# Graph attention, layer 3 in column tiles of TensorE: values in 64 columns, totals in 32

## The chip, the cores and the metric

One core of a Trainium2 chip runs the whole program. The metric is the device time of one execution in microseconds; executions of one kernel agree within about 0.2%. The profile is one execution, with every instruction of every engine.

## The reference

Sixteen independent graphs of 1024 nodes with 256 features go through four layers of graph attention with a layer norm ahead of each and a residual behind. Layers 0 to 2 have one head of 256; layer 3, the one that the change touches, has 4 heads of 64:

```python
weight = sum over types t of (adj == t+1) * (e_src[..., t, :, None] + e_dst[..., t, None, :])
weight = leaky_relu(weight, 0.01)
weight = where(adj == 0, NEG, weight)
attention = softmax(weight, axis=-1)             # per head, 1024 x 1024
dst = einsum('bhij,bhje->bhie', attention, h) + bias
out = relu(dst) + h                              # then a layer norm per head
```

The kernel does not form the softmax. It forms unnormalised weights, multiplies them with the values and with a column that gives their total, and divides afterwards.

## The kernel before

Two batches are in work at a time, as two streams of Python generators. A stream yields an estimate of what it has just traced, and the stream that is behind goes next; the second starts `LAG` later. In layer 3 a stream makes the weights of one head on VectorE (8 tiles of 128 sources x 1024 targets) while TensorE multiplies those of the head before:

```python
EXT = [3, 3, 3, 3 * H]
LAG = 120.0
...
def accumulator(b):                       # in PSUM, two per stream
    return psum.tile([P, HALF], F32, name=f"acc{b % 2}")
...
for n in range(H * NH):                   # 4 heads x 2 halves of 512 targets
    h, g = divmod(n, NH)
    if g == NH - 1:
        behind = weigh3(h + 1)            # VectorE: weights of the next head
        yield from start(behind, b)
    accT = accumulator(b)[: E + 1, :]
    for j in range(NI):                   # 8 blocks of sources
        ...
        nc.tensor.matmul(                 # 64 value columns and the total
            accT, V3[:, j, h, :], weights[h * NI + j][:, ts(g, HALF)],
            start=(j == 0), stop=(j == NI - 1),
        )
        ...
        yield 0.9
    ...
    sums = wide.tile([E + 1, HALF], F32, name="sums")
    nc.scalar.copy(sums, accT)
    ...
    acc = psum.tile([P, NG, E + 1], F32, name="misc")
    for i in range(NG):                   # turn: targets back on partitions
        nc.tensor.transpose(acc[:, i, :], sums[:, ts(i, P)], ident[: E + 1, : E + 1])
    inv = small.tile([P, NG], F32, name="inv4")
    inverse(inv, acc[:, :, E])
    nc.vector.tensor_mul(
        y[:, ts(g, NG), h, :], acc[:, :, :E], inv.unsqueeze(2).to_broadcast([P, NG, E])
    )
```

Of the kernel before, what the change touches and what calls it, by code (L numbers as in the profile page):

```python
# [32 lines left out]
F32 = mybir.dt.float32  # L33
# [8 lines left out]
P = 128  # L42
# [17 lines left out]
def short_path(ctx: ExitStack, tc: tile.TileContext, ins: dict, out: bass.AP, bad: bass.AP):  # L60

    nc = tc.nc
    x, adj = ins["x"], ins["adj"]
    B, N, D = x.shape
    H, T, E = ins["L3_a_src"].shape
    NI = N // P
    NK = D // P
    HALF = 512
    NH = N // HALF
    NG = HALF // P  # L70
    EXT = [3, 3, 3, 3 * H]
    LAG = 120.0

    const = ctx.enter_context(tc.tile_pool(name="const", bufs=1))
    nodes = ctx.enter_context(tc.tile_pool(name="nodes", bufs=3))
    adjs = ctx.enter_context(tc.tile_pool(name="adjs", bufs=4))
    wide = ctx.enter_context(tc.tile_pool(name="wide", bufs=2))
    psum = ctx.enter_context(tc.tile_pool(name="psum", bufs=2, space=bass.MemoryType.PSUM))
    dram = ctx.enter_context(tc.tile_pool(name="dram", bufs=1, space=bass.MemoryType.DRAM))

    ident = const.tile([P, P], F32, name="ident")
# [2 lines left out]
    nc.vector.memset(minus_half, -0.5)  # L84
    ones = const.tile([P, P], F32, name="ones")
    nc.vector.memset(ones, 1.0)

    squares = const.tile([P, B, NI], F32, name="squares")
    inverses = const.tile([P, B, NI], F32, name="inverses")
# [16 lines left out]
    def load(b: int):  # L106


        narrow = narrows[b % 2]
        rows = narrow.bitcast(U8).rearrange("(c t q) j -> c q t j", t=2, q=P)  # L110
        for c in range(NI // 2):
            cast = nc.gpsimd.dma_start(
                rows[c], adj[b, ts(c, 2 * P), :].rearrange("(q t) j -> q t j", t=2)
            )
            tc.keep_in_program_order(cast)
        if b < 2:
            fetch_nodes(b)
        yield

        mask = masks[b] = nodes.tile([P, NI // 2, N, 2], U8, name="mask")  # L120
        for c in range(NI // 2):
            turn = nc.sync.dma_start_transpose(
                mask[:, c].rearrange("p n t -> p (n t)").bitcast(BF), narrow[:, ts(c, P)]
            )
            tc.keep_in_program_order(turn)
            yield
        if b > 1:
            fetch_nodes(b)
            yield
# [20 lines left out]
    small = ctx.enter_context(tc.tile_pool(name="small", bufs=6))  # L150
# [109 lines left out]
    def accumulator(b: int) -> bass.AP:  # L260
        return psum.tile([P, HALF], F32, name=f"acc{b % 2}")
# [54 lines left out]
    def start(behind, b: int):  # L316

        for t in behind:
            if row_taken == [b]:
                return  # L320
            yield t

    def inverse(inv: bass.AP, total: bass.AP):

        nc.vector.tensor_scalar_max(inv, total, TINY)
        nc.vector.reciprocal(inv, inv)  # L326
# [12 lines left out]
    def batch(b: int):  # L339
# [3 lines left out]
        coming = load(b + 2) if b + 2 < B else iter(())  # L343
# [39 lines left out]
        def attend(l: int, V: bass.AP, finish, then: int):  # L383

            weights = []
            behind = weigh(
                b, lambda i: V[:, i, D + 2 : D + 3], lambda j: V[:, j, D + 1 : D + 2],
                ALU.min if l == 1 else ALU.max, weights,
            )
            yield from start(behind, b)  # L390
            following = begin(then) if then < 3 else begin3()
            steps = iter(())
            accs = {}

            def product(i: int, j: int):
                if j == 0:
                    accs[i] = accumulator(b)[:, : D + 1]
                nc.tensor.matmul(  # L398
                    accs[i], weights[j][:, ts(i, P)], V[:, j, : D + 1],
                    start=(j == 0), stop=(j == NI - 1),  # L400
                )


            for j in range(NI):
                next(behind)
                product(0, j)
                product(1, j)
                if b == 0 and j == NI - 1:


                    next(preparing)
                    if l == 0:
                        next(loading[1])
                    next(preparing, None)
                yield 0.9
            for _ in behind:
                pass
            for i in range(NI):
                if i > 1:
                    for j in range(NI):  # L420
                        product(i, j)
                acc = accs.pop(i)
                finish(i, acc)
                if l == 2:
                    next(testing)
                if i != 0:
                    yield 3.6
                if i % 2 == 1:

                    yield from steps  # L430
                    steps = project(b, then, xb, i // 2, following[1])
                yield from islice(steps, 1)
            yield 1.0
            yield from steps
            return following[0]
# [23 lines left out]
        V3 = yield from attend(2, V, finish, 3)  # L459
# [3 lines left out]
        y = single.tile([P, NI, H, E], F32, name="y")  # L463
        normed = []
        shape = [P, NI, E]

        def center(h: int):

            yh = y[:, :, h, :]
            head = ts(h, E)  # L470
            nc.gpsimd.tensor_add(yh, yh, bias[:, head].unsqueeze(1).to_broadcast(shape))  # L471
            nc.vector.scalar_tensor_tensor(yh, yh, 0.0, h3[:, :, head], op0=ALU.max, op1=ALU.add)
            mean = small.tile([P, NI], F32, name="mean")
            nc.vector.tensor_reduce(mean, yh, AX.X, ALU.add)
            nc.vector.tensor_scalar_mul(mean, mean, 1.0 / E)
            nc.vector.tensor_sub(yh, yh, mean.unsqueeze(2).to_broadcast(shape))
            square = wide.tile(shape, F32, name="wide", bufs=1)
            nc.scalar.activation(square, yh, AF.Square)
            var = small.tile([P, NI], F32, name="var")
            nc.vector.tensor_reduce(var, square, AX.X, ALU.add)  # L480
            return yh, head, inverse_root(var, NI, L3_EPS, 1.0 / E)

        def rescale(yh: bass.AP, head, rstd: bass.AP):
            nc.vector.tensor_mul(yh, yh, rstd.unsqueeze(2).to_broadcast(shape))
            nc.gpsimd.tensor_mul(yh, yh, gamma[:, head].unsqueeze(1).to_broadcast(shape))
            nc.gpsimd.tensor_add(yh, yh, xb[:, :, head])

        weights = []

        def weigh3(h: int):  # L490
            if h == H:
                return iter(())
            return weigh(
                b, lambda i: ex[:, i, 2 * H + h : 2 * H + h + 1],
                lambda j: ex[:, j, H + h : H + h + 1], ALU.max, weights,
            )

        behind = weigh3(0)
        yield from start(behind, b)
        for n in range(H * NH):  # L500
            h, g = divmod(n, NH)
            if g == NH - 1:

                behind = weigh3(h + 1)
                yield from start(behind, b)

            accT = accumulator(b)[: E + 1, :]
            for j in range(NI):
                if n == 0:
                    next(behind)  # L510
                nc.tensor.matmul(  # L511
                    accT, V3[:, j, h, :], weights[h * NI + j][:, ts(g, HALF)],
                    start=(j == 0), stop=(j == NI - 1),
                )
                if n > 0:
                    next(behind, None)
                yield 0.9
            for _ in behind:
                pass
            sums = wide.tile([E + 1, HALF], F32, name="sums")  # L520
            nc.scalar.copy(sums, accT)  # L521
            next(coming, None)
            yield 0.5
            acc = psum.tile([P, NG, E + 1], F32, name="misc")
            for i in range(NG):
                nc.tensor.transpose(acc[:, i, :], sums[:, ts(i, P)], ident[: E + 1, : E + 1])  # L526
            inv = small.tile([P, NG], F32, name="inv4")
            inverse(inv, acc[:, :, E])
            nc.vector.tensor_mul(  # L529
                y[:, ts(g, NG), h, :], acc[:, :, :E], inv.unsqueeze(2).to_broadcast([P, NG, E])  # L530
            )
            yield 0.5
            if g == NH - 1:
                if h > 0:
                    rescale(*normed.pop())
                normed.append(center(h))
                yield 1.0
        for _ in coming:
            pass
        rescale(*normed.pop())  # L540
# [8 lines left out]
    def stream(first: int):  # L549
        for _ in loading[first]:  # L550
            yield 2.0
        for b in range(first, B, 2):
            yield from batch(b)
# [3 lines left out]
    next(preparing)  # L557
    streams = [[0.0, stream(0)], [LAG, stream(1)]]
    while streams:
        ahead = min(streams, key=lambda s: s[0])  # L560
        t = next(ahead[1], None)
# [381 lines left out]
```

## Time and profile before

| | before |
|---|---|
| time, median | 3114.9 us |
| TensorE busy | 2982 us (96%) |
| VectorE busy | 2338 us (75%) |
| layer 3's matmuls (line 511), records | 2048, one each 429 ns |
| mean granted clock of TensorE | 0.995 |

The lines behind this table are in the prediction. "Busy" of TensorE rests on modelled ends: successive matmuls overlap in it. To cost TensorE's work one takes the spacing from start to start, not the mean duration. Adding up the starts' spacings by line gives, for before, 1404 us for layers 0 to 2 (line 398), 890 for layer 3 (511), 471 for projections (289), 149 and 129 for two kinds of transposes (282, 306) and 38 for layer 3's turning (526).

### The profile page before, as it was taken

To read this page: it belongs to the slowest core of one execution; us is meant where nothing else is said; L and a number is where in the kernel's file an instruction comes from. 1 tells how busy PE (TensorE), PEld (TensorE's weight loads), DVE (VectorE), ACT (ScalarE), POOL (GpSimd) and SP (SyncE) were. 2 spreads that over 40 slices of the span, in tenths; PEclk is the share of its full clock that TensorE was granted. 3 is DMA by queue.
4 is the path that set the end of the run, shared out by engine and by line. 5 is a ranking of instruction groups with operands and counts; after the bars stand their busy time and mean duration, and the time that the engine had idled before them with its cause. 6 is when DMAs were issued, how large, how long until landed. Compare 5 with 4: busy or idle time off the path is not lost.

```text
span 3112.0 us, 35525 instructions
## 1 busy us (share of the span) xinstructions
PE 2981.7 (96%) x12678; PEld 2047.5 (66%) x12678; DVE 2337.8 (75%) x5234; ACT 737.1 (24%) x1729; POOL 1081.2 (35%) x1405
## 2 busy tenths in 40 slices
PE   7899999999999999999999999999999999999986
PEld 5676756767566675766757667575666767667652
DVE  6678787777877768787786877778777787777856
ACT  1221312223131231312213122231322313122130
POOL 2323433244242333424244242342423434243332
PEclk9999999999999999999999999999999999999998
DMA  8112212022121122111122120221212222001010
GB/s 126 28 28 41 41 14 54 14 41 41 28 44 19 33 41 41 35 20 48 21 41 41 14 54 14 41 41 28 45 15 37 41 35 41 7 28 27 1 28 15
DMA packets 116872, 105.52 MB, mean 34 GB/s; under 512 B 73681, under 2 KB 91217, under 8 KB 116689
## 3 DMA queue, kind: packets, MB, share of 16 engines
q0 software_dynamic: 44256, 81.80, 16.2%
q1 hardware_dynamic: 72432, 21.37, 3.5%
q8 instruction: 103, 1.69, 0.2%
q14 instruction: 81, 0.66, 0.1%
HBM read 153.49 MB, written 33.55 MB: 60 GB/s over the span
## 4 chain that ended last, share of the span: by engine, by line
PE 78%; DVE 15%; POOL 3%; ACT 2%; issue 1%; DMA 1%; SPq 0%; ACTq 0%; POOLq 0%; DVEq 0%
PE acc L398 35%; PE acc L511 25%; PE acc L289 11%; DVE weights L310 8%; PE misc L282 3%; PE row L306 2%; ACT adj_i L141 1%; PE misc L526 1%; POOL y L471 1%; POOL rstd L257 1%; DVE V L355 1%; DVE stats L269 1%; POOL x_b L337 1%; DVE centered L274 1%; ACT below L333 1%
## 5 line engine op out<-in xcount | busy, mean ns | idle before, releaser
L398 PE MATMUL acc<-V,weights 128*128 128x257 f32 x6144 | 1449.3, 383 | 38.0 <-DVE weights L310 29.8
L398 PEld LDWEIGHTS acc<-V,weights 128*128 128x128 f32 x6144 | 1141.6, 190 | 348.6 <-DVE weights L310 100.6
L511 PE MATMUL acc<-weights,V 128*65 128x512 f32 x2048 | 955.9, 592 | 2.0 <-DVE weights L310 1.7
L310 DVE SCALAR_TENSOR_TENSOR weights<-row,ex,mask 128x1024 f32<-128x1024 f32 x512 | 627.8, 1274 | 6.1 <-PE row L306 5.6
L257 POOL TENSOR_TENSOR rstd<-rstd,minus_half 128x2 f32<-128x2 f32 (+1 forms) x320 | 299.5, 936 | 943.1 <-DVE rstd L256 930.7
L289 PE MATMUL acc<-W,hT 128*128 128x259 f32 (+1 forms) x2048 | 515.4, 389 | 26.0 <-ACT hT L284 14.8
L310 DVE SCALAR_TENSOR_TENSOR weights<-row,V,mask 128x1024 f32<-128x1024 f32 x384 | 482.0, 1274 | 46.6 <-PE row L306 46.6
L511 PEld LDWEIGHTS acc<-weights,V 128*65 128x65 f32 x2048 | 273.9, 138 | 361.0 <-issue 312.5
L289 PEld LDWEIGHTS acc<-W,hT 128*128 128x128 f32 x2048 | 379.2, 191 | 138.4 <-ACT hT L284 38.2
L337 POOL TENSOR_TENSOR x_b<-x_b,above 128x256 f32<-128x256 f32 x256 | 196.5, 771 | 427.5 <-DVE above L336 345.1
L333 ACT ACTIVATE below<-acc,inv 128x256 f32<-128x256 f32 x256 | 120.3, 473 | 771.4 <-DVE inv L326 623.6
L269 DVE BATCH_NORM_STATS2 stats<-x_b 128x6 f32<-128x256 f32 x512 | 207.6, 418 | 92.9 <-POOL x_b L337 83.5
L284 ACT COPY hT<-misc 128x512 f32<-128x512 f32 x256 | 146.7, 586 | 344.7 <-PE misc L282 344.6
L471 POOL TENSOR_TENSOR y<-y,bias 128x512 f32<-128x512 f32 x64 | 82.8, 1294 | 406.9 <-DVE y L529 323.5
L274 DVE TENSOR_SCALAR centered<-x_b,mv 128x256 f32<-128x256 f32 x512 | 192.6, 384 | 15.7 <-PE misc L282 12.2
L351 ACT ACTIVATE V<-acc,rstd 128x3 f32<-128x3 f32 x384 | 98.2, 262 | 418.0 <-PE acc L289 418.0
L282 PEld LDWEIGHTS misc<-ident,centered 128*128 128x128 f32 x1024 | 124.1, 141 | 109.7 <-issue 49.0
L282 PE MATMUL misc<-ident,centered 128*128 128x128 f32 x1024 | 162.7, 278 | 31.1 <-DVE centered L274 21.6
L335 DVE TENSOR_SCALAR above<-acc,inv 128x256 f32<-128x256 f32 x256 | 122.5, 481 | 84.4 <-ACT below L333 83.8
L521 ACT COPY sums<-acc 65x512 f32<-65x512 f32 x128 | 74.5, 582 | 409.6 <-PE acc L511 409.6
L355 DVE TENSOR_SCALAR V<-acc,rstd,V 128x256 f32<-128x256 f32 x256 | 133.4, 538 | 37.7 <-ACT V L351 34.9
L141 ACT ACTIVATE adj_i<-adj_i,minus_half 128x1024 bf16<-128x1024 bf16 x128 | 145.8, 1139 | 20.0 <-DMA adj_i<-in_adj_dram 20.0
(69 smaller groups left out, 1870.3 us busy)
## 6 DMA issues: line engine op xcount, KB each, us to landing
adj_i<-in_adj_dram POOLq DMA_DIRECT2D x128, 256.0 KB, 3.9
narrow<-in_adj_dram POOLq DMA_DIRECT2D x64, 256.0 KB, 9.4
out_dram<-y POOLq DMA_DIRECT2D x32, 512.0 KB, 4.3
x_b<-in_x_dram POOLq DMA_DIRECT2D x14, 1024.0 KB, 5.6
x_b<-in_x_dram SPq DMA_DIRECT2D x2, 1024.0 KB, 7.2
mask<-narrow SPq DMA_TRANSPOSE x64, 3.7
W<-in_L_gnn_W_dram SPq DMA_DIRECT2D x3, 256.0 KB, 6.1
weights<-in_L_gnn_a_dram SPq DMA_DIRECT2D x3, 256.0 KB, 7.9
```

The lines of the kernel that those rows point to most:

```text
L141: square = nc.scalar.activation(adj_i, adj_i, AF.Square, bias=minus_half, accum_out=squares[:, b, i : i + 1])
L257: nc.gpsimd.tensor_tensor(r, r, minus_half.to_broadcast([P, n]), op=ALU.pow)
L269: nc.vector.bn_stats(stats, xb[:, 2 * pair + n, :])
L274: nc.vector.tensor_scalar(centered[:, n, :], xb[:, 2 * pair + n, :], mv[:, n, 0:1], 0.0, op0=ALU.subtract, op1=ALU.max,)
L282: nc.tensor.transpose(turned[:, k, ts(n, P)], centered[:, n, ts(k, P)], ident)
L289: nc.tensor.matmul(projected, hT[:, k, ts(n, P)], W[l][:, k, :], start=(k == 0), stop=(k == NK - 1),)
L310: nc.vector.scalar_tensor_tensor(w, r, c(j), masks[b][:, j // 2, :, j % 2], op0=op, op1=ALU.mult)
L333: nc.scalar.activation(below, acc[:, :D], AF.Exp, scale=inv)
L337: nc.gpsimd.tensor_add(xi, xi, above)
L355: nc.vector.tensor_scalar(V[:, i, :D], projected[:, :D], rstd, V[:, i, D : D + 1], op0=ALU.mult, op1=ALU.mult,)
L398: nc.tensor.matmul(accs[i], weights[j][:, ts(i, P)], V[:, j, : D + 1], start=(j == 0), stop=(j == NI - 1),)
L511: nc.tensor.matmul(accT, V3[:, j, h, :], weights[h * NI + j][:, ts(g, HALF)], start=(j == 0), stop=(j == NI - 1),)
```

## The change

Only 65 of the array's 128 columns hold something in line 511. The change divides the array: the 64 value columns go into a tile of 64 columns, and the two halves of targets into the two tiles at once; the one total column is spread over a tile of 32 columns, and two source blocks x two halves go into the four tiles at once. The partial totals of two tiles are added when they are turned, by a small matrix `parts`.

```diff
-    LAG = 120.0
+    LAG = 111.0
+    QUAD = P // 4
...
+    parts = const.tile([P, NH], F32, name="parts")      # picks and adds the four tiles' rows
...
+        for h in range(H):
+            acc = accumulator(b)
+            total = accumulator(b)
+            size = NI if h == 0 else NI // 2
+            for first in range(0, NI, size):
+                for j in range(first, first + size):
+                    if h == 0:
+                        next(behind)
+                    for g in range(NH):
+                        nc.tensor.matmul(
+                            acc[ts(g, E), :], V3[:, j, h, :E], weights[h * NI + j][:, ts(g, HALF)],
+                            start=(j == 0), stop=(j == NI - 1),
+                        )
+                    yield 0.9
...             # (sums = copy of acc; the next head's weights are begun)
+                for j in range(first, first + size, 2):
+                    for n, g in ((n, g) for n in range(2) for g in range(NH)):
+                        nc.tensor.matmul(
+                            total[ts(2 * g + n, QUAD), :],
+                            V3[:, j + n, h, E:].to_broadcast([P, QUAD]),
+                            weights[h * NI + j + n][:, ts(g, HALF)],
+                            start=(j == 0), stop=(j == NI - 2),
+                        )
+                    ...
+                    yield 0.9
...
+            turned = psum.tile([P, NG, NH], F32, name="misc")
             for i in range(NG):
-                nc.tensor.transpose(acc[:, i, :], sums[:, ts(i, P)], ident[: E + 1, : E + 1])
+                nc.tensor.matmul(turned[:, i, :], totals[:, ts(i, P)], parts, start=True, stop=True)
+            inv = small.tile([P, NH, NG], F32, name="inv8")
+            inverse(inv, turned.rearrange("p i g -> p g i"))
+            turned = psum.tile([P, NG, NH, E], F32, name="misc")
+            for i in range(NG):
+                nc.tensor.transpose(
+                    turned[:, i].rearrange("p g e -> p (g e)"), sums[:, ts(i, P)], ident
+                )
...             # (one multiply by inv for both halves)
```

More of the change, by code (lines that the diff above doesn't have):

```diff
@@ L86, in short_path @@
     nc.vector.memset(ones, 1.0)
+    parts = const.tile([P, NH], F32, name="parts")
+    nc.vector.memset(parts, 0.0)
+    for t in range(4):
+        nc.vector.memset(parts[t * QUAD : t * QUAD + 1, t // 2 : t // 2 + 1], 1.0)
     squares = const.tile([P, B, NI], F32, name="squares")
@@ L499, in batch @@
         yield from start(behind, b)
-        for n in range(H * NH):
-            h, g = divmod(n, NH)
-            if g == NH - 1:
-                behind = weigh3(h + 1)
-                yield from start(behind, b)
-            accT = accumulator(b)[: E + 1, :]
-            for j in range(NI):
-                if n == 0:
-                    next(behind)
-                nc.tensor.matmul(
-                    accT, V3[:, j, h, :], weights[h * NI + j][:, ts(g, HALF)],
-                    start=(j == 0), stop=(j == NI - 1),
-                )
-                if n > 0:
+        for h in range(H):
[12 more added lines that the diff above has]
+                    yield 0.9
+                if first + size == NI:
+                    for _ in behind if h == 0 else ():
+                        pass
+                    sums = wide.tile([P, HALF], F32, name="sums")
+                    nc.scalar.copy(sums, acc)
+                next(coming, None)
+                if first == 0:
+                    behind = weigh3(h + 1)
+                    yield from start(behind, b)
+                for j in range(first, first + size, 2):
[6 more added lines that the diff above has]
+                        )
@@ L516, in batch @@
                     next(behind, None)
-                yield 0.9
+                    next(behind, None)
+                    yield 0.9
             for _ in behind:
                 pass
-            sums = wide.tile([E + 1, HALF], F32, name="sums")
-            nc.scalar.copy(sums, accT)
+            totals = wide.tile([P, HALF], F32, name="sums")
+            nc.scalar.copy(totals, total)
             next(coming, None)
             yield 0.5
-            acc = psum.tile([P, NG, E + 1], F32, name="misc")
+            turned = psum.tile([P, NG, NH], F32, name="misc")
@@ L525, in batch @@
             for i in range(NG):
-                nc.tensor.transpose(acc[:, i, :], sums[:, ts(i, P)], ident[: E + 1, : E + 1])
-            inv = small.tile([P, NG], F32, name="inv4")
-            inverse(inv, acc[:, :, E])
+                nc.tensor.matmul(turned[:, i, :], totals[:, ts(i, P)], parts, start=True, stop=True)
+            inv = small.tile([P, NH, NG], F32, name="inv8")
+            inverse(inv, turned.rearrange("p i g -> p g i"))
+            turned = psum.tile([P, NG, NH, E], F32, name="misc")
@@ L529, in batch @@
+            for i in range(NG):
+                nc.tensor.transpose(
+                    turned[:, i].rearrange("p g e -> p (g e)"), sums[:, ts(i, P)], ident
+                )
             nc.vector.tensor_mul(
-                y[:, ts(g, NG), h, :], acc[:, :, :E], inv.unsqueeze(2).to_broadcast([P, NG, E])
+                y[:, :, h, :].rearrange("p (g i) e -> p g i e", g=NH),
+                turned.rearrange("p i g e -> p g i e"),
+                inv.unsqueeze(3).to_broadcast([P, NH, NG, E]),
@@ L531, in batch @@
             )
             yield 0.5
-            if g == NH - 1:
-                if h > 0:
-                    rescale(*normed.pop())
-                normed.append(center(h))
-                yield 1.0
+            if h > 0:
+                rescale(*normed.pop())
+            normed.append(center(h))
+            yield 1.0
         for _ in coming:
```

## The prediction

> **What bounds the kernel now.** I read the page's busy table first, then the strip of 40 slices, the chain that ended last, the costliest groups, and last the timeline of TensorE in a stretch where layer 3 of one stream runs beside layers 0 to 2 of the other.
>
> ```profile
> span 3112.0 us, 35525 instructions
> PE 2981.7 (96%) x12678; PEld 2047.5 (66%) x12678; DVE 2337.8 (75%) x5234; ACT 737.1 (24%) x1729; POOL 1081.2 (35%) x1405
> ...
> PE   7899999999999999999999999999999999999986
> PEclk9999999999999999999999999999999999999998
> ...
> PE 78%; DVE 15%; POOL 3%; ACT 2%; issue 1%; DMA 1%; SPq 0%; ACTq 0%; POOLq 0%; DVEq 0%
> ```
>
> TensorE is at 90% or more in nearly every slice, at full clock, and holds 78% of the chain. Its busy time is modelled, so "96%" alone would not prove it dense; the groups and the timeline do.
>
> ```profile
> L398 PE MATMUL acc<-V,weights 128*128 128x257 f32 x6144 | 1449.3, 383 | 38.0 <-DVE weights L310 29.8
> L511 PE MATMUL acc<-weights,V 128*65 128x512 f32 x2048 | 955.9, 592 | 2.0 <-DVE weights L310 1.7
> L310 DVE SCALAR_TENSOR_TENSOR weights<-row,ex,mask 128x1024 f32<-128x1024 f32 x512 | 627.8, 1274 | 6.1 <-PE row L306 5.6
> L521 ACT COPY sums<-acc 65x512 f32<-65x512 f32 x128 | 74.5, 582 | 409.6 <-PE acc L511 409.6
> ```
>
> L511 is the line that changes. Per batch of 16 it has 4 heads x 2 halves x 8 source blocks = 64 matmuls, 1024 in all, and the page counts 2048: one fp32 matmul is two records. It waits for almost nothing (2.0 us of idle time before it).
>
> ```profile
> 1402.64 1.91 PE L289 MATMUL acc<-W,hT 128*128 128x259 f32 x8
> 1404.39 2.74 PE L511 MATMUL acc<-weights,V 128*65 128x512 f32 x6
> 1406.96 3.63 PE L398 MATMUL acc<-V,weights 128*128 128x257 f32 x16
> 1410.43 0.41 PE L526 MATMUL misc<-ident,sums 65*128 65x65 f32 x4
> 1410.67 1.04 PE L306 MATMUL row<-ident,ex 128*128 128x128 f32 x8
> ```
>
> Six records of L511 take 2.74 us; less one modelled duration of 592 ns, five steps take 2.15 us, so a record costs TensorE 429 ns, not 592. In the same way L398 costs (3.63 - 0.38) / 15 = 217 ns, and a 65-column transpose of L526 (0.41 - 0.226) / 3 = 62 ns. The reader is to see two things: blocks follow each other without a gap (1404.39 + 6 x 0.429 = 1406.96, the very start of L398), so a change of shape costs nothing today; and layer 3 of one stream is cut into short blocks by the other stream. Counting consecutive L511 records in the trace gives 467 blocks for 1024 matmuls, 2.2 matmuls each, most of them of a single matmul. L511 thus holds 2048 x 429 ns = 879 us of TensorE time, 28% of the span.
>
> **What the Trainium skill says.** (1) "FP8 and Floating Point Precision", TensorE Precision Notes: true fp32 takes four passes through the array. The trace agrees: 2 records x 512 columns x 2 passes at the 2.4 GHz that the skill gives is 2 x 427 ns, and 2 x 429 is measured. (2) "TensorEngine Tiling (Array Packing)", Theoretical Speedup and Key Properties: up to 2x with 64 columns and up to 4x with 32, but changing the tiling mode drains TensorE. No trace here shows either: the kernel before runs all its dense work in one mode. (3) "TensorE: Matmul & The Clock Gate", Part 3: three column tiles of 512 moving columns were measured at 2.38x, and matmuls start and end strictly in program order, with no reordering. The trace agrees on the order; it has no tiles. (4) The same page, LDWEIGHTS: the load of the stationary operand scales with its columns (128 take about 107 ns by its rule). The trace agrees: four ordinary fp32 matmuls with 128 stationary and only 14 moving columns (line 240) start 83 to 132 ns apart, mean 118, though streaming 14 columns would take 12 ns.
>
> **The change part by part.**
>
> *Sums and totals.* The 65-column stationary operand is split into 64 value columns and one total. Per head and source block there are two value matmuls (one per half, side by side) and two total matmuls with the one column spread over 32 (four of two blocks side by side). Records rise: 64 + 64 matmuls per batch instead of 64. If tiles run fully side by side, a pair of value matmuls takes the time of one and four totals take the time of one: 32 + 16 = 48 slots of two records instead of 64. That removes 16 slots x 2 x 429 ns = 13.7 us per batch, **220 us** over 16 batches, all from the bound engine.
>
> *Turning.* Removed: 512 transposes at 62 ns, 32 us. Added per head: 4 transposes of 128x128, 256 in all at the 109 ns that the 128-column transposes of L306 show ((1.04 - 0.273) / 7), 28 us; and 4 fp32 matmuls with a 128-column stationary operand and 2 moving columns, 512 records, each bound by its weight load at some 110 ns (line 240 above), 56 us. Net **+52 us** on TensorE.
>
> *Changes of mode.* Layer 3's tiled blocks stand between the other stream's full-width blocks. Before there were 2.2 steps to a block; 768 steps now give about 350 blocks, entered and left: 700 changes. Within layer 3, 64-column and 32-column groups alternate about 14 times per batch, of which 1 - 1/2.2 = 55% fall inside a block: 120 more. What one change costs no trace shows. A lower limit is zero. A natural size for a full drain is what a matmul's modelled duration has beyond its spacing, 592 - 429 = 163 ns[...]. 820 x 163 ns is 134 us; I take 100 ns, **+82 us**, an estimate from the modelled durations, and the softest term.
>
> *Other engines.* ScalarE still makes 128 evictions of 512 columns (582 ns each). VectorE loses 128 groups of a clamp, a reciprocal and a multiply and gains 64 larger ones, some 30 us less of its 2338. Neither is on the chain. VectorE's weights (8 x 1.27 = 10.2 us per head) stay hidden: 2310 us against some 2860 of TensorE. The shorter lag of the second stream (111 for 120) follows half the shortening of a batch and only keeps the streams out of step.
>
> Sum: 220 - 52 - 82 = 86 us off. VectorE's waits may give a little back, but the four clamp-and-reciprocal chains per batch that go away may give as much. About 3020 to 3030 us.
>
> **The rivals.**
>
> *A: the tiles overlap and a change of mode is free.* Then 220 - 52 = 168 us off, 2946 us. For it: today's shape changes cost nothing. Against: the tiling page says in plain words that a mode change drains.
>
> *B: two records per fp32 matmul spoil the overlap.* In program order the queue holds a-high, a-low, b-high, b-low. If starts are strictly in order, b-high cannot start before a-low, and a-low waits for a-high on the same tile. In a long run, pairs still fill two tiles (a-low beside b-high, b-low beside the next a-high): 2x. But four tiles also reach only 2x: eight records in four slots. Then values cost 32 x 2 = 64 record slots and totals 16 x 4 = 64 per batch: 128, exactly as before, plus one slot of run-in per block: 350 x 429 ns = 150 us, plus the turning and the changes of mode: 3114 + 150 + 52 + 82 = about 3400, or 3270 if the run-in and the drain hide one another and half the blocks merge. For it: the measured order in the skill, the two records in the trace. Against: the skill's figures are for one record per tile; a tile with a place for one waiting instruction would let b-high pass.
>
> *C: tiles do not overlap in fp32 at all.* 256 record slots instead of 128: +879 us, near 4000. The skill names no such limit for fp32 matmuls (only for transposes); I give it 5%.
>
> *D: full overlap with heavy changes of mode.* A drain plus an exposed load of weights, say 163 + 100 ns each: 820 x 263 = 216 us, and 220 - 52 - 216 leaves -48: 3160 us.
>
> **Range and chances.** I give overlap without trouble (A to the central estimate) about 45%, overlap eaten by changes of mode 25%, rival B 25%, C 5%. The 2% line lies at 62 us. So faster by over 2%: 0.43; within 2%: 0.24; slower by over 2%: 0.33. I predict 3020 us with a range of 2925 to 3290, wide upward because B is a real possibility and downward closed by the sum of A.
>
> **What would show it.** In the profile of the changed kernel:
> - The value matmuls' spacing inside a block: 4 records per 858 ns (overlap), per 1290 and then 858 (B), or per 1716 (C). For totals: 8 records per 858 ns (overlap) or per 1716 (B).
> - The start of the first full-width record after a tiled block: at the last slot's end (free), or 100 to 260 ns later (drain). The same on entering.
> - The turning matmuls with 2 moving columns: near 110 ns apart, not 25.
> - The chain of waits should still be TensorE at above 70%, and VectorE above 75% of a shorter span.
> I am wrong if a record of a tile cannot run beside the second record of another (then the time is above 3200), if changes of mode cost over 250 ns (then nothing is gained), or if VectorE's weights become the wait that ends the idle time before layer 3's matmuls for more than some 30 us.

## The result, and the profile after

The changed kernel takes **3197.5 us** (3196.3 to 3199.3, 4 runs) against 3114.9: 1.0265 times as long, 95% interval 1.0247 to 1.0283. I had predicted 3020 us, in a range of 2925 to 3290: the direction was forecast wrongly.

The page of the kernel after, with the busy table, the chain by engine and the two groups that replace line 511 (columns: line, engine, operation, operands, count, busy us, mean ns, idle before):

```profile
PE 3046.0 (95%) x14982; PEld 2012.2 (63%) x14982; DVE 2293.9 (72%) x5047; ACT 733.4 (23%) x1729; POOL 1092.3 (34%) x1405
...
PE 81%; DVE 13%; POOL 3%; ACT 1%; issue 1%; DMA 1%; SPq 0%; ACTq 0%; POOLq 0%; DVEq 0%
...
L519 PE MATMUL acc<-weights,V 128*64 128x512 f32 x2048 | 542.9, 609 | 2.5 <-DVE weights L317 1.5
...
L536 PE MATMUL acc<-weights,V 128*32 128x512 f32 x2048 | 347.8, 602 | 0.0
```

TensorE is still the bound (81% of the chain), and it is busier, not idler. Lines 519 and 536 together have twice the records of line 511, so they overlap; but by start-to-start spacing they take 520 + 335 = 855 us, only 34 less than 890. The timeline of TensorE in the kernel after (start, length in us, line, count of records) shows why:

```profile
1401.14 1.06 PE L536 MATMUL acc<-weights,V 128*32 128x512 f32 x8
1402.14 1.08 PE L519 MATMUL acc<-weights,V 128*64 128x512 f32 x4
1403.15 1.06 PE L536 MATMUL acc<-weights,V 128*32 128x512 f32 x6
1404.13 1.94 PE L519 MATMUL acc<-weights,V 128*64 128x512 f32 x8
1406.00 1.04 PE L536 MATMUL acc<-weights,V 128*32 128x512 f32 x2
1406.98 1.07 PE L519 MATMUL acc<-weights,V 128*64 128x512 f32 x2
1407.98 1.09 PE L313 MATMUL row<-ident,V 128*128 128x128 f32 x8
```

Three things are to be seen.

*The overlap is real.* At 1401.14 eight records, that is four fp32 total matmuls, are through after 1.00 us, hardly more than one matmul's 0.86 (two records of 429 ns). Record by record, the four first records of the tiles start 7 ns apart, and 0.45 us later the four second records do. Rival B of the prediction is out. (Whether the second record of one tile waits in place or stands behind the others in the queue cannot be told from this trace.)

*Groups are torn.* At 1403.15 there are 6 records, three totals, and at 1406.00 there are 2, one total that takes 0.98 us all by itself. At 1406.98 a single value matmul takes 1.00 us without its partner. The scheduler, which orders instructions when the program is built, did not keep the four or the pair together. An extract of the built order (lines 519 are values, 536 totals; one program row each, x2 for two alike):

```
L519 Matmult acc_5683<-weights_5685,V 64x512 x2
...
L536 Matmult acc_5684<-weights_5685,V 32x512          <- one total of a four
L519 Matmult acc_5683<-weights_5689,V 64x512 x2
L536 Matmult acc_5684<-weights_5685,V 32x512          <- the other three
L536 Matmult acc_5684<-weights_5689,V 32x512 x2
```

In the trace I counted as one slot all starts of a block within 300 ns of one another. Whole groups need 1536 slots (16 batches x 48 x 2 records) of 429 ns; the trace has **1770**, of which 136 hold a value matmul's record without a partner, 164 one total and 160 three. The extra 234 slots are 100 us, so the gain in slots is not 220 us but (2048 - 1770) x 0.429 = 119 us.

*Each change of mode has a gap.* The first matmul after a change starts 93 ns later than it would without one (522 ns instead of 429 after a tiled record; 310 instead of 217 after a full-width one). Then the second slot of the new block starts late too: by 51 ns with 64 columns, 24 with 32, 104 with 128 (50 to 57 for transposes). I read this as a weight load that is no longer hidden: it grows with the stationary columns, and at 1402.14 the first load of the block starts with its first matmul, where in the kernel before, at 1404.39, it starts 0.22 us ahead. There are 902 changes: 84 us of gaps and, weighted by the kinds of blocks, some 46 us of exposed loads, about 130 us.

Turning grew from 38 to 87 us on TensorE, +48. The sum -119 + 130 + 48 = +59 us, and TensorE's idle time (all its gaps, from the records) grew from 108 to 126 us, +18: +77 of the 84 us of the span. Counted by starts, what comes later than slots and changes call for grew by as much (177 to 196 us), and this growth lies in stretches that the trace's clock records show at half clock (7 to 26 us). The mean granted clock fell from 0.995 to 0.989, and 0.6% of the span is 19 us: the clock has a part in the loss, but a small one.

### The profile page after: what moved, and what is told of

The parts are those of the page before. It is cut to its first block, busy times and chain, and to the rows that moved or that the text cites. A ratio compares the mean times of both kernels' runs of the same rounds, so it can differ in the third digit from the quotient of the medians. Undisturbed runs are those within 1.5% of the kernel's fastest.

```text
span 3196.5 us, 40092 instructions
## 1 busy us (share of the span) xinstructions
PE 3046.0 (95%) x14982; PEld 2012.2 (63%) x14982; DVE 2293.9 (72%) x5047; ACT 733.4 (23%) x1729; POOL 1092.3 (34%) x1405
## 4 chain that ended last, share of the span: by engine, by line
PE 81%; DVE 13%; POOL 3%; ACT 1%; issue 1%; DMA 1%; SPq 0%; ACTq 0%; POOLq 0%; DVEq 0%
PE acc L405 38%; PE acc L519 16%; PE acc L296 11%; PE acc L536 9%; DVE weights L317 6%; PE misc L289 3%; PE row L313 2%; PE misc L553 1%; POOL rstd L264 1%; DVE V L362 1%; POOL y L478 1%; DVE above L342 1%; DVE y L561 1%; DMA adj_i<-in_adj_dram 1%; DVE mean L481 1%
## 5 line engine op out<-in xcount | busy, mean ns | idle before, releaser
L317 DVE SCALAR_TENSOR_TENSOR weights<-row,ex,mask 128x1024 f32<-128x1024 f32 x512 | 635.3, 1277 | 83.3 <-PE row L313 57.8
L296 PE MATMUL acc<-W,hT 128*128 128x259 f32 (+1 forms) x2048 | 532.1, 395 | 34.4 <-DVE V L362 18.4
L264 POOL TENSOR_TENSOR rstd<-rstd,minus_half 128x2 f32<-128x2 f32 (+1 forms) x320 | 312.8, 979 | 726.4 <-DVE rstd L263 615.1
L519 PE MATMUL acc<-weights,V 128*64 128x512 f32 x2048 | 542.9, 609 | 2.5 <-DVE weights L317 1.5
L536 PE MATMUL acc<-weights,V 128*32 128x512 f32 x2048 | 347.8, 602 | 0.0
L519 PEld LDWEIGHTS acc<-weights,V 128*64 128x64 f32 x2048 | 127.5, 136 | 301.4 <-issue 258.7
L281 DVE TENSOR_SCALAR centered<-x_b,mv 128x256 f32<-128x256 f32 x512 | 209.6, 415 | 3.5
L536 PEld LDWEIGHTS acc<-weights,V 128*32 128x32 f32 x2048 | 56.6, 107 | 203.5 <-issue 202.6
```

Of the source, the lines that this page charges most:

```text
L264: nc.gpsimd.tensor_tensor(r, r, minus_half.to_broadcast([P, n]), op=ALU.pow)
L281: nc.vector.tensor_scalar(centered[:, n, :], xb[:, 2 * pair + n, :], mv[:, n, 0:1], 0.0, op0=ALU.subtract, op1=ALU.max,)
L296: nc.tensor.matmul(projected, hT[:, k, ts(n, P)], W[l][:, k, :], start=(k == 0), stop=(k == NK - 1),)
L317: nc.vector.scalar_tensor_tensor(w, r, c(j), masks[b][:, j // 2, :, j % 2], op0=op, op1=ALU.mult)
L519: nc.tensor.matmul(acc[ts(g, E), :], V3[:, j, h, :E], weights[h * NI + j][:, ts(g, HALF)], start=(j == 0), stop=(j == NI - 1),)
L536: nc.tensor.matmul(total[ts(2 * g + n, QUAD), :], V3[:, j + n, h, E:].to_broadcast([P, QUAD]), weights[h * NI + j + n][:, ts(g, HALF)], st ...
```

## The experiments

The theory from the trace: torn groups (about 100 us) and changes of mode (about 130 us) eat the 220 us. Rivals: the stage is bound by waits, for VectorE's weights or the shared `row` buffer, so slots saved come back as idle time; or the turning or the new lag is to blame.

### e4: only the changes of mode

Kernel before, with one tile of 64 columns instead of 65: as many matmuls, no pairs, nearly the old order; the total is replaced by a one. Its output is wrong, which doesn't matter for the time.

```diff
-            accT = accumulator(b)[: E + 1, :]
+            accT = accumulator(b)[:E, :]
-                    accT, V3[:, j, h, :], weights[h * NI + j][:, ts(g, HALF)],
+                    accT, V3[:, j, h, :E], weights[h * NI + j][:, ts(g, HALF)],
-            nc.scalar.copy(sums, accT)
+            nc.gpsimd.memset(sums[E : E + 1, :], 1.0)
+            nc.scalar.copy(sums[:E, :], accT)
```

> The kernel before with 64 columns in layer 3 instead of 65 (the total is dropped and a one stands in for it: wrong result on purpose). No pairs, no turning of totals, as many matmuls and nearly the same order as before, but each block of layer 3 now is in another tiling mode: 935 changes. If a change of mode costs 145 ns on the mean (93 ns of drain and 25 to 104 ns of an exposed weight load, as read in the trace after): 3114 + 135 = about 3250 us. If changes of mode are free and only torn groups cost: 3114 us.

Measured: 3254.3 us, ratio 1.0444 (1.0427 to 1.0461), that is +139.8 us for 935 changes: **149.5 ns each**. From the timeline of this kernel:

```profile
1411.15 1.04 PE L306 MATMUL row<-ident,ex 128*128 128x128 f32 x8
1412.11 3.65 PE L511 MATMUL acc<-weights,V 128*64 128x512 f32 x8
1415.69 2.02 PE L289 MATMUL acc<-W,hT 128*128 128x259 f32 x8
```

The block of eight takes from 1412.11 to 1415.69, 3.58 us, where 8 x 0.429 = 3.43: the missing 0.15 is 51 + 93 ns. By the starts alone, gaps and late second slots add up to 152 us here; 140 reach the time. The cost of a change is shown with no overlap and no torn group in play, and the rival "changes are free" is out.

### e5: only the groups kept whole

Kernel after; the second of a pair and the last three of a four have first claim in the scheduler once the first is issued.

```diff
+                        with tc.high_priority() if g > 0 else nullcontext():
                             nc.tensor.matmul(acc[ts(g, E), :], ...
+                        with tc.high_priority() if n + g > 0 else nullcontext():
                             nc.tensor.matmul(total[ts(2 * g + n, QUAD), :], ...
```

> The kernel after, with one difference: the second value matmul of a pair and the last three totals of a group of four have first claim once the first of them is issued. Nothing waits in order that did not before. Built order: every pair and every four whole, 785 changes of mode (903 after). Theory (torn groups are part of the loss): 1536 slots instead of 1770, -100 us, 118 fewer changes at 145 ns, -17 us: 3080 us. Rival (as the pinned kernels hint: what is saved in slots comes back as idle time of TensorE, because VectorE's weights or the shared row buffer bound this stage): 3180 us or more.

Measured: 3106.1 us, ratio 0.9973 (0.9956 to 0.9989): **91 us below the kernel after**, from a change of order alone. The trace has 1536 slots (from 1770), all pairs and fours whole, and 784 changes (from 902). Its timeline:

```profile
1402.10 1.94 PE L520 MATMUL acc<-weights,V 128*64 128x512 f32 x8
1403.96 0.44 PE L289 MATMUL misc<-ident,centered 128*128 128x128 f32 x2
1404.33 1.06 PE L538 MATMUL acc<-weights,V 128*32 128x512 f32 x8
1405.33 1.15 PE L296 MATMUL acc<-W,hT 128*128 128x259 f32 x4
1406.40 1.06 PE L538 MATMUL acc<-weights,V 128*32 128x512 f32 x8
```

Counts are multiples of 4 (pairs) and 8 (fours). The saving expected was 117 us; TensorE's idle time rose from 126 to 141 us, so part of it came back as idle time, but not, as the rival has it, most of it.

### e1 to e3: groups pinned to the traced order

My first means of keeping groups whole was another: each tiled matmul is pinned behind everything traced before it on TensorE.

```diff
-                        nc.tensor.matmul(
+                        tc.keep_in_program_order(nc.tensor.matmul(
```

e1 does just this; e2 also yields only at the end of a chunk (for values from head 1 on); e3 also makes a chunk a whole head (`size = NI`).

> Every tiled matmul of layer 3 is pinned behind what was traced before it on TensorE, so no pair and no group of four is torn by the scheduler. Built order: all groups whole, 687 changes of mode instead of 903. Theory (torn groups and changes of mode cost the gain): 1770 slots of 429 ns become 1536, -100 us, and 216 fewer changes at about 145 ns, -31 us: 3197 - 131 = 3066 us. Rival (the time is set by waits for VectorE's weights or by the turning, not by the order on TensorE): 3170 to 3200 us, with as much idle time of TensorE more as busy time less.

> As e1_pin_all, and a chunk of four value steps or two total steps gives way to the other stream only at its end. Built order: groups whole, 497 changes. Theory: 190 fewer changes than e1_pin_all at 145 ns, -28 us: about 3040 us. Rival (changes of mode cost nothing, only torn groups do): equal to e1_pin_all. Second rival (long blocks starve the other stream's engines): slower than e1_pin_all.

> As e2_pin_coarse with a whole head's eight value steps in one block and its totals in another. Built order: 361 changes. Theory on TensorE alone: 136 fewer changes than e2, -20 us: about 3020 us. Rival: the next head's weights can only start once the totals of the head are through, so TensorE waits for VectorE (8 x 1.27 us per head) and the time is equal to e2 or above it.

Measured: e1 3234.6 us (1.0388), e2 3191.3 (1.0240), e3 3135.3 (1.0060). All three missed my numbers by over 100 us. Groups were whole (1536 slots in all three) and changes fell to 686, 496 and 360, as built; but idle time of TensorE rose from 126 to 239, 222 and 184 us. Who waited for whom on TensorE in e1 (total us, times, longest):

```profile
PE row L313 <- DVE weights L317: 72.7, 17, 4.9
PE acc L405 <- DVE weights L317: 53.7, 34, 2.4
...
PE acc L519 <- DVE weights L317: 12.8, 15, 1.5
```

Line 313 fills the one `row` buffer that both streams share; it must wait until VectorE has made the last weights from the row before. Of its 73 us, 71 stand before rows of layers 0 to 2 (`row<-ident,V`). In the kernel after, TensorE had other work placed there (there the list of waits shows no wait of line 313 for weights). A pin to *everything* traced before also ties the two streams to one another, and with the order fixed TensorE stands. The mean granted clock fell too, to 0.963 in e1 against 0.989 after. The trace's clock records know only full and half clock: half clock holds for 241 us in e1 (190 in e2, 79 in e3), 74 in the kernel after and 32 before, and in e1 mostly for 10.2 or 13.7 us at a time, beginning within a long wait. One such place, with half clock from 1025.2 to 1035.5:

```profile
1027.29 1.97 PE L313 MATMUL row<-ident,V 128*128 128x128 f32 x8 [4.86 <-DVE weights L317]
1031.65 5.61 PE L405 MATMUL acc<-V,weights 128*128 128x257 f32 x16 [2.39 <-DVE weights L317]
```

At full clock eight and sixteen such records took 1.04 and 3.63 us. A pin thus costs twice: the wait, and the slow clock seen after it (that the wait sets off the slow clock no run tests). So the rival is right in kind about pinned order, though e1 is slower still than its 3170 to 3200 us, and e5 shows that it is the pins that do it, not the whole groups. From e1 to e3 the fall in time goes with fewer changes, less idle time and less time at half clock together; these are not separated there.

### e6 and e7: order inside the stream, then whole chunks

e6 adds to e5 an ordering edge from each tiled matmul to the one before it in its own stream; e7 also gives a chunk's matmuls after its first one first claim.

```diff
+                        behind_last(m)        # edge to the stream's previous tiled matmul
-   with tc.high_priority() if g > 0 else nullcontext():
+   with tc.high_priority() if g > 0 or j > first else nullcontext():          # e7, likewise for totals
```

> As e5_followers, and the tiled matmuls of a stream keep their own order among themselves (totals no longer float ahead of values), with no tie to the other stream's. Built order: 707 changes. Theory: 78 fewer changes than e5, -11 us: 3069 us. Rival: order kept inside the stream makes waits, as pinning did: above e5.

> As e6_chain, and all matmuls of a chunk after its first have first claim, so a chunk of four value steps or two total steps runs through unless its weights are not there. Built order: 512 changes. Theory: 195 fewer changes than e6, -28 us: about 3040 us. Rival: idle time grows by as much, 3080 us or more.

Measured: e6 3100.4 us (0.9956), between its two expectations, e7 3098.8 (0.9946), a time such as its rival expected. Changes fell to 706 and 511 as built, but e7's expected 28 us did not come; it differs from e6 by less than the intervals. In both, some 120 slots inside blocks come late, 32 us together (1 us in e5), nearly all of them values of head 0: its weights come from VectorE one each 1.28 us, a step of TensorE takes 0.86, and the order that holds back the totals leaves the gap unfilled. That is what e6 loses against e5; fewer changes and less spacing of line 405 (1418 to 1398 us) outweigh it. Why e7's 195 fewer changes (29 us at 149.5 ns) brought nothing over e6 shows in the list of waits: the transposes ahead of the projections (line 289) wait for VectorE's `centered` 44 times, 44.6 us, where in e6 it was 5 times, 7.5 us. The sum of idle time (141 to 144 us) hides this twice: other waits shrank, and a start up to 163 ns late leaves no gap behind a modelled end. Counted by starts, what comes later than slots and changes call for grows from 221 to 251 us, as much as the changes saved. That the long chunks hold VectorE's work up is likely, and not tested.

### e8 and e10: the turning

The totals are turned by transposes (one record of 109 ns each) and added by VectorE, instead of by fp32 matmuls with two moving columns (two records of 112 ns, as the prediction took from line 240 and the trace after confirms). e8 is e7 with this, e10 is e5 with this.

```diff
-            turned = psum.tile([P, NG, NH], F32, name="misc")
+            turned = psum.tile([P, NG, P], F32, name="misc")
             for i in range(NG):
-                nc.tensor.matmul(turned[:, i, :], totals[:, ts(i, P)], parts, start=True, stop=True)
+                nc.tensor.transpose(turned[:, i, :], totals[:, ts(i, P)], ident)
...
+            nc.vector.tensor_reduce(
+                inv, turned.rearrange("p i (g n q) -> p g i n q", g=NH, n=2)[:, :, :, :, 0], AX.X, ALU.add
+            )
```

> As e7_chunk, and the totals are turned by four transposes of 109 ns per head and a small add on VectorE instead of eight records of 112 ns. TensorE: -(8 x 112 - 4 x 109) ns x 64 = -29 us against e7_chunk; VectorE +64 x 0.2 us. Theory: e7 - 25 us. Rival (TensorE is no longer the bound): equal to e7_chunk.

> As e5_followers with the totals turned by transposes (as in e8): sizes the turning alone on an order that is otherwise the same (789 changes against 785). Theory: 64 x (8 x 112 - 4 x 109) ns = 29 us less on TensorE, which is the bound here: 3106 - 29 = 3077 us. Rival: hidden: 3106 us.

Measured: e8 3081.8 us (0.9895), 17 us below e7; e10 3102.6 us (0.9964), only 3.5 below e5, which is within the intervals. In e10 the turning takes 66 us of TensorE by spacing instead of 87 (21 of the 29 us meant), but idle time rises from 141 to 153 us. TensorE at 94 to 95% busy is no longer the only limit: of 29 us of work taken from it, at most 17 reach the time. The granted clock moved the other way in the two pairs (half clock 67 to 91 us from e5 to e10, 71 to 52 from e7 to e8), so the difference between 3.5 and 17 is not the order alone.

### e9, e11, e12: head 0 and the lag

e9 is e8 with order and first claim of chunks from head 1 on only. e11 is the kernel after with `LAG = 120.0`. e12 is e8 with `LAG = 120.0`.

> As e8_chunk_turn, but in head 0, whose weights come from VectorE one every 1.27 us, only groups are kept whole and totals may float into the gaps between values; order and first claim of whole chunks hold from head 1 on. Built order: groups whole, 623 changes (512 in e8). In e6 to e8 some 122 steps of head 0 stood inside a block and waited for weights, 32 us in all. Theory: those 32 us go, 111 more changes cost 16 us: e8 - 16 = about 3066 us. Rival: the waits only move to another line: equal to e8, 3082 us.

> The kernel after with the second stream's lag at 120 as before, instead of 111: undoes that part of the change alone. It shifts how the two streams meet, so the built order differs: 997 changes against 903, 216 torn single matmuls or more as before. If the lag only keeps the streams out of step: within 1% of 3197 us, above it by about 94 x 145 ns = 14 us. If the new lag is what made the kernel slow: back toward 3114 us.

> As e8_chunk_turn with the second stream's lag at 120 as before. Built order: groups whole, 614 changes (512 in e8), so by changes alone 15 us more: 3097 us. In e11 the longer lag took 9 us off the kernel after, with idle time of TensorE 21 us less, although there were 94 changes more. If that carries over (the lag sets how well the two streams fill each other's gaps): 3070 us or less.

Measured: e9 3082.4 us (0.9902), equal to e8. The late slots inside blocks fell from 33 to 9 us as meant, but 110 more changes (16 us at 149.5 ns) took most of that. e11 3188.5 us (1.0239): the new lag is not what made the kernel slow; if anything 120 is better by some 9 us, where 14 us more had been expected (the 1% holds), with 996 changes and 1748 slots, groups as torn as before. e12: **3058.9 us, 0.9818 (0.9805 to 0.9831)**, the best of all, 1.8% below the kernel before and so just short of the 2% line, and 23 us below e8 in spite of 101 more changes; TensorE's idle time is 132 us against 159. The groups of TensorE in e12:

```profile
L405 PE MATMUL acc<-V,weights 128*128 128x257 f32 x6144 | 1465.8, 387 | 17.0 <-DVE above L342 7.0 <-DVE weights L317 4.9 <-DVE x_b L447 1.1
...
L531 PE MATMUL acc<-weights,V 128*64 128x512 f32 x2048 | 487.1, 604 | 5.8 <-DVE weights L317 4.7
L550 PE MATMUL acc<-weights,V 128*32 128x512 f32 x2048 | 242.8, 597 | 0.0
```

Idle time before line 405 is 17 us, where e8 has 68 and the kernel after 62 (before line 296 it grew, from 23 in e8 to 61), and the late slots inside blocks fell from 33 us in e8 to 4. The lag chooses which parts of the two streams meet; its effect was found by trying, not foreseen, and the kernel before was tried with no other lag.

| kernel | median us | ratio | slots | changes | TensorE idle us |
|---|---|---|---|---|---|
| before | 3114.9 | 1 | 2048 | 1 | 108 |
| after | 3197.5 | 1.0265 | 1770 | 902 | 126 |
| e4, one tile, changes alone | 3254.3 | 1.0444 | 2048 | 935 | 102 |
| e1, pinned | 3234.6 | 1.0388 | 1536 | 686 | 239 |
| e5, groups whole | 3106.1 | 0.9973 | 1536 | 784 | 141 |
| e8, chunks, transposes | 3081.8 | 0.9895 | 1536 | 512 | 159 |
| e12, e8 with lag 120 | 3058.9 | 0.9818 | 1536 | 613 | 132 |

(The last three columns are counted from the trace records; idle time is the sum of all gaps of TensorE.)

## Why the prediction was wrong

- **"48 slots of two records instead of 64 ... That removes ... 220 us."** This is the step that failed. It took the order in the source for the order on the engine, and no rival questioned it. The tiles do overlap fully, but the built order tears groups, which costs 234 more slots, and the gain is 119 us. Of the 169 us between the 86 saved by the prediction and the 83 lost, this is 101; the changes of mode are 48, idle time and a slower clock 18. e5 shows it as a cause: whole groups with nothing pinned give back 91 us. The profile before did not show it: its 467 blocks for 1024 matmuls may come from the `yield` after every matmul as well as from the scheduler. The built order of the new kernel, which needs no chip, would have.
- **"820 x ... 100 ns, +82 us."** The mechanism was right and the size too small. The count was near (902), the cost was 149.5 ns in e4, of which 93 ns is the gap and the rest the exposed weight load. I had set the load aside for rival D. At the measured figures the term is about 130 us instead of 82. Even with whole groups the change would then have been worth 220 - 130 - 52 = 38 us by this sum; e5, with fewer changes but more idle time, got 8.
- **Turning, "+52 us".** Right: +48 on TensorE, with 112 ns per record of the two-column matmuls. But a cost on a bound engine is not the same as time: e10 took 21 us of it away by spacing, and the time fell by 3.5, within the intervals.
- **Rivals.** A (free changes) fell with e4. B (no overlap of two-record matmuls) fell with the 7 ns between the tiles' starts. C (no overlap in fp32) fell with the same. D gave the nearest time (3160 us) by a cost per change that is too high, 263 ns, without torn groups. The sign that I named, over 30 us of waits for VectorE's weights before layer 3's matmuls, appeared in no run by idle time (1.5 us after, at most 16, in e8; the late slots of e6 to e8, 32 us, come near it); in the pinned kernels the long waits stand before the rows and matmuls of layers 0 to 2.
- **The lag "only keeps the streams out of step".** Nearly so in the kernel after (e11: 9 us), but with whole chunks going back to 120 was worth 23 us (e12).
- **Two readings are off**, without effect on the sum: line 240's four records are two fp32 matmuls and start 111 to 132 ns apart, not 83 to 132 (the mean of 118 is right); and TensorE's 2982 us less the 86 of the sum are some 2900, not 2860.
- **The signs that I listed** were the useful part: spacing inside a block, the start after a block and the spacing of two-column matmuls each answered one step. A list that included the number of records per block would have caught the failed step as well.

## What to carry to other kernels

Instructions that gain only by standing side by side have to be held together by something stronger than their order in the source: look at the built order before judging the idea, and bind the members to one another, not to everything around them, since a full pin (e1) saved 100 us of slots and brought 113 us more idle time and 167 us more at half clock. Count the changes of tiling mode that an interleaved schedule will make and charge each with its gap and with the weight load that it uncovers; here tiling saves at best 0.43 us per block of sources (220 us over 512 blocks), which three changes at 0.15 us use up, and the kernel after makes 1.8 changes per block. When the bound engine gets lighter, re-tune how the streams meet (here the lag, 23 us) before judging the change.

## What the Trainium skill lacked or had wrong

- "TensorEngine Tiling (Array Packing)", Key Properties, says that changing the mode drains TensorE and gives no size. Here a change costs 93 ns of gap for each of the pairs of 128, 64 and 32 columns, plus 24 to 104 ns by which the second slot is late, read as a weight load that is no longer hidden; 149.5 ns of time on the mean over 935 changes (e4).
- "TensorE: Matmul & The Clock Gate", Part 3, gives about 4 ns from tile to tile and 2.38x for three column tiles. Here four fp32 tiles of 512 columns start 7 ns apart, and eight records pass in 2 slots of 429 ns inside a block: near 4x, before the change of mode is paid (a lone group of four with one change takes 1.00 us, 3.4x).
- No page says how fp32 matmuls, two records each in this trace, behave in column tiles. Here the first records of all tiles of a group start together and the second ones together, 0.43 to 0.48 us later.
